# Column numbers of the count compares moved to PSUM, and layer 2's passes, row loads and way home paced anew, in a three-layer graph network kernel

## The chip, the cores and the metric

The kernel runs on one core of a Trainium2 chip. The metric is the device time of one execution in microseconds. The kernel before takes 2138.58 us (median of 3 runs, 2134.11 to 2144.74).

## The reference

A graph has 6250 nodes with 256 features and 100,000 edges, sorted by destination; every node also has an edge to itself. Three graph convolutions (256 to 512, 512 to 512, 512 to 256 features) each end in a relu. The input is added to the result, and each row is normalised.

```python
loops = jnp.arange(n)
src = jnp.concatenate([edge_index[0], loops]); dst = jnp.concatenate([edge_index[1], loops])
deg = segment_sum(ones_like(dst), dst, n)
dinv = where(deg > 0, rsqrt(deg), 0.0)
norm_edge = dinv[src] * dinv[dst]
for W, b in ((W1, b1), (W2, b2), (W3, b3)):
    h = relu(segment_sum((h @ W)[src] * norm_edge[:, None], dst, n) + b)
return layernorm(x + h)
```

## The kernel before, in words

The nodes are cut into 50 blocks (`NB`) of 125 (`Q`). A layer sums the rows of each block's sources in one of two ways.

**Gathered blocks.** GpSimd issues one indirect DMA per step (L1380, `room<-tab`): up to 128 rows of the layer's table in DRAM land in one buffer of a ring. A gathered block takes 14 "round" steps and 3 "beyond" steps, and some steps are shared by two or ten blocks. VectorE adds round rows to a running total (L1441). Beyond rows are split into a high and a low half by ScalarE (L1433) and VectorE (L1436), and TensorE multiplies them by a selection matrix (L1396).

**Dense blocks.** A 125 x 125 matrix of edge counts per pair of blocks is multiplied with the block rows that stay in SBUF (`parts`). In layers 1 and 3 the dense matmuls stand in L1464, behind a conversion of the counts from bytes (`converted`, L1348, on ScalarE and some on VectorE). In layer 2 the first 16 blocks are dense: four passes of four blocks each ("teams", L1193) run over all 50 block rows. Every unit of a pass needs the row halves (L1170 on ScalarE, L1172 on VectorE) and the counts, converted from bytes that SP reads back from DRAM (`room<-kept`, converted in L1160).

**The counts** are made in layer 1 (and for the last six blocks in layer 3) by `counts`. For four slots of 128 edges at a time VectorE compares slot values with column numbers: two instructions in L1041, one that writes 500 elements (125 node numbers, for two pairs of slots) and one that writes 1000 (250 keys). TensorE multiplies the two results (L1114), and ScalarE turns the sum into bytes (L1076). The column numbers (`runs`: each number twice, 16 bits each) lie in SBUF. Two steps go by per group of four slots.

**The finder** (`found_rounds`, `found_beyond`) works out, also during layer 1, which row each lane of a gather fetches. Its matmuls (L589, L598, L635, L647, L649) write columns 256 to 511 of the PSUM bank `near_cols`, and ScalarE reads them there (L593, L602, L637, L652). In layer 1 nothing uses columns 0 to 255 of that bank.

**Order.** All engines run in the order in which the program was written, without reordering. `layer` writes it step by step: the gather of this step, the work on rows gathered 3 to 6 steps earlier, the steps of finished blocks (`after1`, `after2`, `after3`), then a list of side jobs (`extras`), each a generator that says after how many steps it wants to go on, and then the dense matmuls that are due. Layer 1 has 423 steps, layer 2 599 and layer 3 317. The side jobs of layer 1 include the finder, then `counts`, then `caching`. `caching` brings layer 2's table rows into `parts`, two blocks per load (25 loads on SP); it begins when the dense blocks of layer 1 are finished, goes on while layer 1 drains, and then takes one load per step of layer 2.

**Layer 2's side jobs.** `teams` gives one yield per `PACE[1] / PACE[0]` parts of a unit: four parts (one per block, two matmuls each) per unit, 200 units. Twelve yields (`FRONT`) are taken ahead. A block that is finished goes through two matrix products (`after2`, L1594 and L1614) and is stored to `tab2`; as long as the teams run, it is not kept in SBUF, because `parts` still holds layer 2's rows. `home` brings these rows into `parts` when the teams have ended: runs of up to four blocks are loaded by SP (`parts<-tab`), and two turns later ScalarE and VectorE split them (L1220, L1222). When layer 2 drains, `ahead_of_time` puts 45 matmuls of layer 3's first dense block between (L1251).

```python
        for n in range(len(runs) + 2):
            if n < len(runs):
                b, e = runs[n][0], runs[n][-1] + 1
                by_rows(nc.sync, parts[:, b:e, C:].bitcast(F32), tables[2][b * Q:e * Q, :]...)
```

`by_rows` makes two DMAs of every load or store, one of 112 rows and one of 13.

Of the kernel before, what the change touches and what calls it, by code (L numbers as in the profile page):

```python
# [10 lines left out]
F32 = mybir.dt.float32  # L11
F32R = mybir.dt.float32r
BF16 = mybir.dt.bfloat16
# [10 lines left out]
P = 128  # L24
# [24 lines left out]
EXTRA = 0  # L49
TEAM = 4  # L50
TEAMS = 4
PACE = (2, 3)
FRONT = 12
MANY = 32
ALONE = 2
# [8 lines left out]
G = 5  # L64
# [3 lines left out]
RUN = 2  # L68
# [5 lines left out]
def by_rows(queue, tile_rows, dram_rows, store=False):  # L74

    for s in (slice(0, EVEN), slice(EVEN, Q)):
        if store:
            queue.dma_start(out=dram_rows[s], in_=tile_rows[s])
        else:
            queue.dma_start(out=tile_rows[s], in_=dram_rows[s])  # L80
# [320 lines left out]
def sorted_path(ctx: ExitStack, tc: tile.TileContext, x, edges, starts, found, wts, biases, room, late, out):  # L401
# [14 lines left out]
    nc = tc.nc  # L416
# [4 lines left out]
    N, C = x.shape  # L421
    HID = w1_sb.shape[2]
    EC = d.shape[1]
    NB = N // Q
# [328 lines left out]
    with tc.tile_pool(name="sdeg1", bufs=1) as dp1, tc.tile_pool(name="sdeg", bufs=2) as dp, \  # L753
# [26 lines left out]
        keys = const.tile([P, G * NB], BF16, name="keys")  # L780
# [183 lines left out]
    HW = -(-WIDE * (Q + G * NB) // 2 // 4) * 4  # L964
    hot_rooms = [room[:, 3 * MW + n * HW:][:, :HW].bitcast(BF16)[:, :WIDE * (Q + G * NB)] for n in range(HOMES)]
    first_rows = [room[:, at:at + C] for at in range(3 * MW + HOMES * HW, room.shape[1] - 4 * C - C + 1, C)]
    runs = room[:, room.shape[1] - 4 * C:][:, :G * NB * RUN // 2].bitcast(BF16).rearrange("p (v w) -> p v w", w=RUN)
    b1_rows = room[:3, room.shape[1] - 3 * C:][:, :C].bitcast(BF16)
    turned = [room[:, room.shape[1] - n * C:][:, :KC * Q].rearrange("p (k v) -> p k v", v=Q) for n in (2, 1)]
    pair = KH * 2 * Q  # L970
# [9 lines left out]
    def totals_of(stack, name, width, n_of):  # L980

        pool = stack.enter_context(tc.tile_pool(name=name, bufs=1))
        return [pool.tile([P, width], F32, name=f"total{n}") for n in range(n_of)]
# [11 lines left out]

    split = split_rows_of(one, "sfirst_split", 0, C)
    totals = totals_of(one, "sfirst_totals", C, 3)
    nc.vector.tensor_copy(runs, keys.unsqueeze(2).to_broadcast([P, G * NB, RUN]))
    bias_left = work.tile([Q, HID], F32, name="szs")[:3]
    nc.sync.dma_start(out=bias_left, in_=bass.AP(tensor=b1.tensor, offset=b1.offset, ap=[[0, 3], [1, HID]]))  # L1000

    ps_cols = ctx.enter_context(tc.tile_pool(name="sps_cols", bufs=1, space=bass.MemoryType.PSUM))
    near = ps_cols.tile([P, 512], F32, name="near_cols")
    ps_sum = ctx.enter_context(tc.tile_pool(name="sps_sum", bufs=1, space=bass.MemoryType.PSUM))
    accs = [ps_sum.tile([P, HID], F32, name=f"sacc{n}") for n in range(3)]
    mm_bank = ps_sum.tile([P, HID], F32, name="smm")
# [123 lines left out]
    stored, cached, at_home = set(), set(), set()  # L1130
# [3 lines left out]
    def caching():  # L1134

        while finished < FEW:
            yield 1
        for p in range(NB // 2):
            k = order[2 * p]
            while not {k, k + 1} <= rows_made:  # L1140
                yield 1
            by_rows(nc.sync, parts[:, k:k + 2].bitcast(F32), tables[1][k * Q:(k + 2) * Q, :].rearrange("(b p) c -> p b c", p=Q))
            cached.update((k, k + 1))
            yield 1

    def teams(groups):

# [34 lines left out]
        for u, (g, k) in enumerate(units):  # L1182
            for n, b in enumerate(groups[g]):
# [12 lines left out]
                if u % NB == NB - 1:  # L1196
                    team_ended[0](b, team_banks[n], f"team{n}")
                pace += PACE[0]
                while pace >= PACE[1]:
                    pace -= PACE[1]  # L1200
                    yield 1
        teams_done = True

    def home():

        while not teams_done:
            yield 1
        runs = []
        for b in sorted(waiting):
            if runs and runs[-1][-1] == b - 1 and len(runs[-1]) < 4:  # L1210
                runs[-1].append(b)
            else:
                runs.append([b])
        for n in range(len(runs) + 2):
            if n < len(runs):
                b, e = runs[n][0], runs[n][-1] + 1
                by_rows(nc.sync, parts[:, b:e, C:].bitcast(F32), tables[2][b * Q:e * Q, :].rearrange("(b p) c -> p b c", p=Q))
            if n >= 2:
                to = slice(runs[n - 2][0], runs[n - 2][-1] + 1)
                nc.scalar.copy(parts[:, to, :C], parts[:, to, C:].bitcast(F32))  # L1220
                yield 1
                nc.vector.tensor_sub(parts[:, to, C:], parts[:, to, C:].bitcast(F32), parts[:, to, :C].bitcast(F32))  # L1222
                at_home.update(runs[n - 2])
            yield 1

    rows_made = set()
# [451 lines left out]
    def other_parts():  # L1678
        for g, h in ((GRP, PIECE), (0, 0), (0, PIECE), (GRP, 0)):
# [5 lines left out]
            yield 1  # L1685

    loading = caching()
    team_work = teams([every[g * TEAM:(g + 1) * TEAM] for g in range(TEAMS)])
    def the_rest_found():
# [8 lines left out]
    def last_weights():  # L1698
# [11 lines left out]
    totals = totals_of(two, "swide_totals", HID, 2)  # L1710
    layer(1, HID, TEAM * TEAMS, [], after2, wide_rows,
          extras=[(5, last_weights()), (0, loading), (0, team_work), (20, home()), (steps(TEAM * TEAMS) - 2 * KF, fetch_first())],
          filler=ahead_of_time())
    assert begun % PIECE == 0
# [9 lines left out]
    runs = pairs.tile([P, G * NB, RUN], BF16, name="runs")  # L1724
# [6 lines left out]
def kernel(ctx: ExitStack, tc: tile.TileContext, x, edges, dst, w1, b1, w2, b2, w3, b3, out):  # L1731
# [133 lines left out]
    with tc.If(n_other == 0) as cmp:  # L1865
        sorted_path(tc, x, edges, starts, (d, nxt, ones, line, more, ends, other), (w1_sb, w2_sb, w3_sb), (b1, b2_sb, b3),
                    room, (load_x, late_w, load_w2, load_w3), out)
# [43 lines left out]
```

## Time and profile before

| | |
|---|---|
| profiled execution, its own time | 2139.47 us |
| its span, first to last instruction | 2137.7 us |
| median of 3 runs | 2138.58 us |
| layer 1: first gather to last gather issued | 105.6 to 771 us |
| layer 2 | 820.5 to 1671.3 us |
| layer 3 and the end | 1696.4 to 2137.7 us |
| busy: TensorE, VectorE, ScalarE, GpSimd | 86%, 73%, 54%, 70% of the span |

A profile's rows name source line, engine, operation, the tile written and those read. "POOL" is GpSimd, "DVE" VectorE, "ACT" ScalarE, "PE" TensorE (its weight loads "PEld"), "SP" the engine that issues most loads. In the table of stretches each engine's busy time is followed by its number of instructions, then come the granted TensorE clock (1.00 is full), the mean busy share of the DMA engines and GB/s. In rows of groups, the numbers behind the bar are the busy time, the mean duration of one in ns and the idle time of the engine before it. In rows of time, the first number is the start and the second the time taken, and brackets hold the idle time before.

### The profile page before, as it was taken

The numbers are of one execution on the slowest core, as the hardware profiler recorded it, in microseconds if no ns is written. First come the engines' busy times: TensorE is split into PE (matmuls) and PEld (weight loads), VectorE is DVE, ScalarE is ACT, GpSimd is POOL, SyncE is SP. The second block draws the span as 40 slices with busy tenths as digits, with TensorE's granted clock in tenths as the row PEclk, the third lists the DMA queues.
The fourth block names the chain that finished last, engine by engine and source line by source line (L and its number), as shares of the span: only waits on it lengthen the run. The fifth ranks groups of instructions, "written<-read, shape, count | busy, mean of one in ns | idle before, by whom it ended". The sixth has DMA issues, their size and how long they took to land. (4 is left out here: it accounts for less than half of the span.)

```text
span 2137.7 us, 29525 instructions
## 1 busy us (share of the span) xinstructions
PE 1840.7 (86%) x8487; PEld 1392.6 (65%) x8487; DVE 1565.7 (73%) x3299; ACT 1155.1 (54%) x2272; POOL 1503.1 (70%) x1382
## 2 busy tenths in 40 slices
PE   2548888989989995598999999999968799999996
PEld 1336655656656663476887787787756577777775
DVE  5699888878877733577668767767777378888877
ACT  0658767867867763344445444444443355555552
POOL 2088878877877734577777767777777477777775
PEclk6559999999999997799999999999988899999998
DMA  7434444444444549877767767777797467777884
GB/s 151 135 87 145 134 125 143 141 137 143 140 142 141 163 138 265 231 223 221 222 198 229 216 195 214 219 216 209 224 269 222 132 184 201 209 205 198 209 214 134
DMA packets 189676, 391.26 MB, mean 183 GB/s; under 512 B 43661, under 2 KB 105748, under 8 KB 189502
## 3 DMA queue, kind: packets, MB, share of 16 engines
q0 software_dynamic: 84816, 255.18, 42.3%
q1 hardware_dynamic: 88846, 122.24, 20.4%
q10 hardware_dynamic: 15840, 11.86, 2.3%
q8 instruction: 68, 1.11, 0.2%
q14 instruction: 106, 0.87, 0.1%
HBM read 332.12 MB, written 57.00 MB: 182 GB/s over the span
## 5 line engine op out<-in xcount | busy, mean ns | idle before, releaser
L1380 POOL DMA_INDIRECT room<-tab,round_src x1064 | 1166.0, 1096 | 439.3 <-issue 171.4
L1441 DVE TENSOR_TENSOR total<-total,room 125x256 f32<-125x256 f32 (+1 forms) x1030 | 551.7, 536 | 122.0 <-DMA room<-tab,round_src 107.1
L1348 ACT CAST piece<-room 125x625 fp32r<-125x625 uint8 x477 | 341.9, 725 | 110.6 <-PE win_ps L1464 28.8
L1380 POOL DMA_INDIRECT room<-tab,over_src x266 | 303.4, 1141 | 108.4 <-issue 43.3
L1172 DVE TENSOR_TENSOR both<-parts,both 125x512 fp32r<-125x512 f32 x200 | 137.9, 690 | 185.7 <-ACT both L1170 183.6
L1170 ACT CAST both<-parts 125x512 fp32r<-125x512 f32 x200 | 123.8, 619 | 269.8 <-PE smm L1193 269.2
L1464 PE MATMUL win_ps<-parts,piece 125*125 125x512 f32 x900 | 250.6, 417 | 0.5 <-ACT piece L1348 0.5
L1041 DVE TENSOR_TENSOR room<-room,slots 128x500 bf16<-128x500 bf16 (+1 forms) x326 | 247.9, 801 | 1.1 <-PE mat_ps L1114 1.1
L1433 ACT CAST halves<-room 128x256 fp32r<-128x256 f32 (+1 forms) x275 | 137.1, 504 | 177.6 <-DMA room<-tab,over_src 127.5
L1436 DVE TENSOR_TENSOR halves<-room,halves 128x256 fp32r<-128x256 f32 (+1 forms) x275 | 145.8, 541 | 94.4 <-ACT halves L1433 92.2
L1464 PE MATMUL smm<-parts,piece 125*125 125x512 f32 x705 | 193.4, 417 | 5.0 <-DVE piece L1348 5.0
L1193 PE MATMUL sacc<-both,team_piece 125*125 125x512 f32 x400 | 139.5, 425 | 64.2 <-ACT team_piece L1160 33.2
L1396 PE MATMUL sacc<-halves,shot 128*125 128x512 f32 x475 | 158.2, 430 | 39.1 <-ACT halves L1433 20.8
L1464 PE MATMUL mat_ps<-parts,piece 125*125 125x512 f32 x700 | 191.3, 413 | 0.0
L1464 PEld LDWEIGHTS win_ps<-parts,piece 125*125 125x125 f32 x900 | 160.7, 190 | 46.9 <-issue 12.1
L1114 PEld LDWEIGHTS <-room 128*125 128x125 bf16 x650 | 87.4, 144 | 107.4 <-issue 56.0
L1464 PEld LDWEIGHTS smm<-parts,piece 125*125 125x125 f32 x705 | 126.4, 191 | 36.5 <-DVE piece L1348 5.4
L1464 PE MATMUL sacc<-parts,piece 125*125 125x512 f32 x450 | 148.6, 444 | 0.0
L1464 PEld LDWEIGHTS mat_ps<-parts,piece 125*125 125x125 f32 x700 | 122.9, 187 | 35.5 <-issue 8.2
L1396 PEld LDWEIGHTS sacc<-halves,shot 128*125 128x125 f32 x475 | 93.4, 199 | 78.1 <-DVE halves L1436 31.0
L1160 ACT CAST team_piece<-room 125x500 fp32r<-125x500 uint8 x200 | 121.1, 605 | 38.2 <-DMA room<-kept 38.2
L1193 PE MATMUL mat_ps<-both,team_piece 125*125 125x512 f32 x400 | 134.9, 419 | 0.6 <-DVE room L1555 0.6
(416 smaller groups left out, 3306.3 us busy)
## 6 DMA issues: line engine op xcount, KB each, us to landing
kept<-room SPq DMA_DIRECT2D x32, 683.6 KB
room<-kept SPq DMA_DIRECT2D x32, 683.6 KB
room<-tab,round_src POOLq DMA_INDIRECT x1064
parts<-tab SPq DMA_DIRECT2D x34, 448.0 KB
tab<-st SPq DMA_DIRECT2D x58, 224.0 KB
room<-kept SPq DMA_DIRECT2D x160, 68.4 KB
room<-in_x SPq DMA_DIRECT2D x50, 112.0 KB
out<-st ACTq DMA_DIRECT2D x50, 112.0 KB
```

Of the source, the lines that this page charges most:

```text
L1041: nc.vector.tensor_tensor(out, runs[:, :shape[2], :shape[3]].unsqueeze(1).to_broadcast(shape), numbers.rearrange("p (s w) -> p s w", w=sha ...
L1160: nc.scalar.copy(team_pieces[u % 2], used_in[u // PIECE % 2][:, :, u % PIECE, :])
L1170: nc.scalar.copy(to[:, :HID], row)
L1172: nc.vector.tensor_sub(to[:, HID:], row, to[:, :HID].bitcast(F32))
L1193: nc.tensor.matmul(team_banks[n][:Q], lhsT=team_pieces[u % 2][:, n, :], rhs=both_parts[u % 2][:, h * HID:(h + 1) * HID], start=(u % NB == ...
L1348: convert(piece, made_or_read[:, c * PIECE:(c + 1) * PIECE, :])
L1380: nc.gpsimd.indirect_dma_start(out=row, out_offset=None, in_=tables[i], in_offset=bass.IndirectOffsetOnAxis(ap=at, axis=0))
L1396: nc.tensor.matmul(acc[:Q, :size], lhsT=hots[b][:, k], rhs=two[:, c0:c0 + size], start=(k == c0 == 0), stop=(k == BEYOND + 1 and c0 + size ...
L1433: nc.scalar.copy(two[:, :width], landed[chunk - hi_lag])
L1436: nc.vector.tensor_sub(two[:, width:], landed.pop(chunk - lo_lag), two[:, :width].bitcast(F32))
L1441: nc.vector.tensor_add(own, parts[:, b].bitcast(F32) if i == 1 and r == 0 else own, landed.pop(chunk - ADDED[i])[:Q])
L1464: nc.tensor.matmul(acc_d[:Q], lhsT=got[done // PIECE][:, k % PIECE, :], rhs=parts[:, k], start=(k == 0), stop=(k == NB - 1))
```

## The change

Three things are changed.

1. Before layer 1, the doubled column numbers are written to SBUF as before and then copied as 250 words of 32 bits to columns 0 to 249 of `near_cols`. Layer 1's compares (now L1043) take their first input from there. Their second input and their output stay in SBUF. Layer 3's compares are as before.
2. Layer 2's teams yield at 8/11 instead of 2/3 per part, and from the fifth load on `caching` waits four steps instead of one.
3. `home` goes through one run per step instead of two steps, and splits a run four turns after its load instead of two. A wait of one step between the split's two halves is gone.

```diff
-PACE = (2, 3)
+PACE = (8, 11)
...
-    runs = room[:, room.shape[1] - 4 * C:][:, :G * NB * RUN // 2].bitcast(BF16).rearrange("p (v w) -> p v w", w=RUN)
...
-    nc.vector.tensor_copy(runs, keys.unsqueeze(2).to_broadcast([P, G * NB, RUN]))
+    ps_cols = ctx.enter_context(tc.tile_pool(name="sps_cols", bufs=1, space=bass.MemoryType.PSUM))
+    near = ps_cols.tile([P, 512], F32, name="near_cols")
+    runs_room = room[:, room.shape[1] - 4 * C:][:, :G * NB]
+    nc.vector.tensor_copy(runs_room.bitcast(BF16).rearrange("p (v w) -> p v w", w=RUN), keys.unsqueeze(2).to_broadcast([P, G * NB, RUN]))
+    nc.vector.tensor_copy(near[:, :G * NB], runs_room)
+    runs = near[:, :G * NB].bitcast(BF16).rearrange("p (v w) -> p v w", w=RUN)
...
-    ps_cols = ctx.enter_context(tc.tile_pool(name="sps_cols", bufs=1, space=bass.MemoryType.PSUM))
-    near = ps_cols.tile([P, 512], F32, name="near_cols")
...
@@ caching
             cached.update((k, k + 1))
-            yield 1
+            yield 1 if p < 4 else 4
@@ home
-        for n in range(len(runs) + 2):
+        for n in range(len(runs) + 4):
             if n < len(runs):
...
-            if n >= 2:
-                to = slice(runs[n - 2][0], runs[n - 2][-1] + 1)
+            if n >= 4:
+                to = slice(runs[n - 4][0], runs[n - 4][-1] + 1)
                 nc.scalar.copy(parts[:, to, :C], parts[:, to, C:].bitcast(F32))
-                yield 1
                 nc.vector.tensor_sub(parts[:, to, C:], parts[:, to, C:].bitcast(F32), parts[:, to, :C].bitcast(F32))
-                at_home.update(runs[n - 2])
+                at_home.update(runs[n - 4])
             yield 1
```

## Prediction

> **What bounds the kernel now.** I read the table of stretches first, with one stretch per stage; the bounds differ between them. In order: layer 1 while the finder runs, the rest of layer 1, its drain, layer 2's start (two rows), its long middle, its steps after the teams, its drain, layer 3.
>
> ```profile
> 105.60:560.00 454.40, 385.66 (x2102) 263.88 (x2103) 390.46 (x938) 331.76 (x697) 365.18 (x284) 0.92 0.45 132
> 560.00:771.00 211.00, 193.53 (x822) 130.45 (x822) 154.75 (x315) 151.83 (x287) 166.80 (x146) 0.95 0.51 149
> 771.00:820.50 49.50, 31.25 (x119) 20.70 (x117) 3.40 (x8) 15.80 (x28) 0.67 (x1) 0.87 0.65 169
> 820.50:890.40 69.90, 38.49 (x139) 28.73 (x140) 30.23 (x47) 22.43 (x40) 36.05 (x35) 0.74 0.93 261
> 890.40:950.00 59.60, 55.38 (x234) 44.11 (x233) 46.13 (x72) 30.41 (x56) 45.79 (x45) 0.95 0.73 209
> 950.00:1563.60 613.60, 589.93 (x2628) 475.78 (x2628) 448.13 (x703) 297.89 (x562) 459.36 (x442) 0.99 0.75 216
> 1563.60:1671.30 107.70, 76.42 (x322) 61.76 (x320) 76.64 (x118) 34.36 (x65) 82.00 (x77) 0.84 0.85 241
> 1671.30:1696.40 25.10, 23.11 (x99) 17.45 (x99) 5.28 (x10) 10.70 (x20) 1.06 (x1) 0.81 0.39 108
> 1696.40:2137.70 441.30, 408.84 (x1796) 320.01 (x1795) 348.45 (x879) 224.92 (x410) 330.98 (x317) 0.97 0.72 191
> ```
>
> In layer 1 no engine looks full, so I asked for GpSimd's groups there (first three rows) and in layer 2's middle (last three).
>
> ```profile
> L1380 POOL DMA_INDIRECT room<-tab,round_src x336 | 406.0, 1208 | 125.3 <-issue 36.3 <-DVE parts L891 21.7 <-DVE room L1041 20.4
> L1380 POOL DMA_INDIRECT room<-tab,over_src x84 | 114.0, 1357 | 27.1 <-issue 8.2 <-DVE total L1441 6.1 <-DVE room L1041 5.2
> L1380 POOL DMA_INDIRECT room<-tab,rest x3 | 4.0, 1348 | 0.9 <-DVE room L1041 0.6 <-DVE ebegin L609 0.3
> ...
> L1380 POOL DMA_INDIRECT room<-tab,round_src x351 | 365.5, 1041 | 119.5 <-issue 84.2 <-DVE total L1441 15.9 <-DMA room<-tab,round_src 6.1
> L1380 POOL DMA_INDIRECT room<-tab,over_src x88 | 90.8, 1032 | 33.8 <-issue 21.0 <-DVE total L1441 9.1 <-DMA room<-tab,round_src 2.4
> L1380 POOL DMA_INDIRECT room<-tab,rest x3 | 3.0, 1002 | 0.9 <-issue 0.6 <-DMA room<-tab,round_src 0.3
> ```
>
> A gather takes 1239 ns on average in layer 1 (524.0 us over 423), 1039 in layer 2 (459.3 over 442). The rows in order of time show why. First VectorE and GpSimd around 641 us, then a pair from layer 2:
>
> ```profile
> 640.91 1.52 DVE L1041 TENSOR_TENSOR room<-room,slots 128x500 bf16<-128x500 bf16 x2
> 643.15 1.52 DVE L1041 TENSOR_TENSOR room<-room,slots 128x500 bf16<-128x500 bf16 x2
> 647.75 0.43 DVE L1436 TENSOR_TENSOR halves<-room,halves 128x256 fp32r<-128x256 f32 x1 [0.95 <-ACT halves L1433]
> 641.32 1.93 POOL L1380 DMA_INDIRECT room<-tab,over_src  x1 [0.30 <-DVE room L1041]
> 643.56 1.93 POOL L1380 DMA_INDIRECT room<-tab,over_src  x1 [0.30 <-DVE total L1441]
> 647.06 0.95 POOL L1380 DMA_INDIRECT room<-tab,over_src  x1 [0.31 <-DVE room L1067]
> ...
> 1095.65 0.74 DVE L1548 SCALAR_TENSOR_TENSOR szs<-sacc,sdinv,total 125x512 f32<-125x512 f32 x1
> 1096.13 0.95 POOL L1380 DMA_INDIRECT room<-tab,round_src  x1 [0.31 <-issue]
> ```
>
> A gather that begins while VectorE is idle takes 0.95 us and has 0.30 us before it. One that begins inside a compare (641.32, 643.56), which reads two inputs in SBUF, takes 1.93: it goes on when the compare ends. One that begins inside an instruction with one large input in PSUM and one in SBUF (1096.13, inside L1548) takes 0.95. So layer 1 is GpSimd's: 423 gathers at 0.95 + 0.30 are 529 us, the excess is 524 - 402 = 122, together 651 of the 666 us from 105.6 to 771. Layer 2's middle has GpSimd's chain (459.4 + 442 x 0.30 = 592 of 613.6 us) and TensorE (590) side by side at 96%.
>
> **Part 1, layer 1.** How much of the 122 us is the compares'? In layer 2's middle, with other two-input work and no compare, the excess is 459.3 - 442 x 0.95 = 39 us, 0.09 per gather; over 423 gathers 38. The compares have 122 - 38 = 84, at most 122. I take 85: 70 before 560 us (279 gathers), 15 after (144).
>
> How long the compares themselves take from PSUM no row shows. The nearest rows:
>
> ```profile
> L1041 DVE TENSOR_TENSOR room<-room,slots 128x1000 bf16<-128x1000 bf16 x162 | 193.5, 1194 | 0.0
> L1041 DVE TENSOR_TENSOR room<-room,slots 128x500 bf16<-128x500 bf16 x163 | 67.5, 414 | 1.1 <-PE mat_ps L1114 1.1
> L1441 DVE TENSOR_TENSOR total<-total,room 125x512 f32<-125x512 f32 x442 | 304.5, 689 | 46.3 <-DMA room<-tab,round_src 39.2
> L1441 DVE TENSOR_TENSOR total<-total,room 125x256 f32<-125x256 f32 x588 | 247.2, 420 | 75.6 <-DMA room<-tab,round_src 67.9 <-DMA total<-tab 1.8
> L1627 DVE TENSOR_TENSOR st<-str,sdinv 125x256 f32<-125x256 f32 x15 | 5.7, 417 | 0.0
> ```
>
> 256 elements from PSUM take what they take from SBUF (417, 420). From 256 to 512 elements the f32 rows grow by 269 ns, 1.05 ns each: 500 elements would take 676 at that rate, but the short compare takes 414, so it runs two elements at a time; the long one (1194 for 1000) runs one. Bounds from PSUM: 414 or 676 for the short, 676 or 1194 for the long. I take both unchanged, by the PSUM row that costs the same as SBUF's. At 676 the short ones add 163 x 0.26 = 43 us of VectorE work; at 676 the long ones remove 162 x 0.52 = 84. The Trainium skill, "VectorE: DVE Perf Modes", section "The perf-mode tier table (the rule you actually need)", gives tensor_tensor with any PSUM operand one element per cycle, while the section "Why PSUM operands drop a tier" below it still allows a packed rate of two. No 16-bit PSUM input is in this trace; the first sentence makes it a rival.
>
> What is late once the 85 us go? Before 560 us GpSimd's chain falls to 454 - 70 = 384, while VectorE has 390 us of work and TensorE 386. Layer 2's 96% on 390 gives 407. After 560, GpSimd falls to 196 and TensorE's 193.5 at 96% are 202, so -9.
>
> The change also adds waits. The columns share a bank with the finder's matmuls, and the built program guards by bank: counted in it, 75 compares wait for a ScalarE read of `near_cols`, 35 for a matmul into it, and 73 matmuls or weight loads of the finder wait for a compare. The compares are in VectorE's queue, with the adds (L1441) behind them that free gather buffers; the finder's matmuls hold the dense matmuls behind them. Where it is tightest, compare, matmul, ScalarE read and next compare form a ring per two steps:
>
> ```profile
> L635 PE MATMUL near_cols<-emarks,elow 128*128 128x256 bf16 x34 | 9.8, 289 | 16.9 <-DVE emarks L630 16.8
> L637 ACT ACTIVATE epast<-near_cols,eless 128x256 bf16<-128x256 f32 x34 | 16.4, 483 | 25.7 <-PE near_cols L635 25.6
> L1348 ACT CAST piece<-room 125x625 fp32r<-125x625 uint8 x477 | 341.9, 725 | 110.6 <-PE win_ps L1464 28.8
> ```
>
> 0.41 + 1.19 + 0.29 + 0.48 = 2.37 us, with half a cast (0.36) ahead of ScalarE's read 2.73. Two steps take 2 x 454.4 / 279 = 3.26 now and 2.92 at 407. The ring fits, barely; I charge 0.1 us for each of the 110 waits, some 12 us (bounds 0, and a whole cast each, 80). So 407 + 12 = 419, or -35. The one added copy to PSUM is under half a microsecond. Layer 1: -35 - 9 = **-44**. Its drain keeps its loads and stores: 0.
>
> **Part 2, layer 2.** At the start SP's loads of `parts` crowd out the teams' counts:
>
> ```profile
> 842.43 34.29 SPq L80 DMA_DIRECT2D parts<-tab  x16
> 881.01 56.35 SPq L80 DMA_DIRECT2D room<-kept  x40
> 888.38 1.22 PE L1193 MATMUL sacc<-both,team_piece 125*125 125x512 f32 x2 [22.42 <-ACT team_piece L1160]
> 890.45 1.28 POOL L1380 DMA_INDIRECT room<-tab,over_src  x1 [18.59 <-DVE total L1441]
> ```
>
> TensorE loses 22 us and GpSimd 19. Spread over 48 steps instead of 12, the 13 loads let the counts through. But up to 890 the DMA engines were 93% busy at 261 GB/s; the same bytes must pass, so only the idle time behind the loads' end (842.43 + 34.29 = 877) can come back. I take -8 (bounds -18 and 0).
>
> The middle: 800 parts at 8/11 instead of 2/3, less the 12 taken ahead, put the teams' last matmul into step 571, not 522. TensorE gets 2.75 instead of 3 of their matmuls per step, GpSimd's chain stays at 592 / 442 = 1.34 us per step. The step goes from 1.388 to about 1.36: 442 x 0.028 = -12 (bounds 0 and -21), and the 49 steps that had 107.7 / 77 = 1.40 give -2.
>
> The end: after the teams 28 steps are left instead of 77. `home` brings 42 blocks of 128 KB in 11 of them.
>
> ```profile
> parts<-tab SPq DMA_DIRECT2D x34, 448.0 KB
> ```
>
> With 0.45 MB per large load and 0.26 MB per gather (128 rows of 2 KB), the last 28 steps move 7.3 + 5.4 + 0.8 (first counts of layer 3) = 13.5 MB; at 241 to 261 GB/s (the stretch after the teams, and layer 2's start) that is 52 to 56 us, against 28 x 1.40 = 39 now: +14 (bounds 0, if the gathers wait less than the bytes say, and +17). Cover there is none: ScalarE and VectorE wait for these loads. The teams' last blocks now go through their matrix products while the layer drains; counted in the built program, 44 instead of 20 matmuls of L1594 and 16 instead of 8 of L1614.
>
> ```profile
> L1594 PE MATMUL win_ps<-room,w_sb 128*128 128x250 f32 x352 | 81.4, 373 | 0.0
> L1614 PE MATMUL str<-w,room 128*125 128x256 f32 x184 | 43.4, 379 | 0.5 <-ACT room L1605 0.5
> ```
>
> 24 x 0.23 + 8 x 0.24 = +7, as TensorE is 92% busy there; I take +6. Layer 2: -8 - 12 - 2 + 14 + 6 = **-2**.
>
> **The sum.** Against the profiled execution's own 2139.5 us: -44 - 2 = -46, 2093.5. The median is 0.9 lower: **2093 us**. About 0.5% (10.7 us) is what a measurement of this kernel can tell from no change.
>
> **Rivals.** (a) The short compares run one element at a time. VectorE's work before 560 us becomes 390 + 28 (two thirds of the 43, by its share of the time) = 418, at 96% and with the ring 447, -7; after it -9 stays: layer 1 -16, total 2121. Against it: L1627 reads PSUM at SBUF's pace. 17%.
>
> (b) The long compares run two at a time. Then GpSimd and TensorE bound: TensorE's 386 at 96% are 402 before 560 us, -52; with -9 and -2 that is 2076, and with layer 2 at its better bounds (-18 - 21 - 2 + 6) 2043. Nothing in the rows says why the long one is slow. 10%.
>
> (c) The compares are not what holds GpSimd. Layer 1 stays, the time is 2139 - 2 = 2137. The Trainium skill, "SBUF — State Buffer", section "Who interferes with whom", says that two SBUF inputs contend with GpSimd's reads, but reports a probe in which tensor_tensor did not stall DMAs issued by GpSimd. By the probe the sum would be -2, by the rows at 641 us it is -46. The trace decides against the probe: 9%.
>
> (d) Slower: the ring decides. It does from 3.26 us per two steps on, the present pace. If the gather's rows come late to ScalarE (L1433 stands in the same queue) or casts pile up, 3.6 us on 110 pairs are 110 x 0.34 = +37; with -9 and layer 2's -2 that is +26, 2165. For it: ScalarE already waits for the finder's matmuls (25.7 us before L637). Against it: each engine's other work per two steps (2.8 us) fits beside the ring. 14%.
>
> (e) Layer 2's burst costs more than the start and middle give: +30 there and -44 in layer 1, 2125. 5%.
>
> **How the numbers follow.** The forecast has 45%, at 2065 to 2125. Range: the lower end 2050 takes in most of (b); the upper end 2140 takes in (a), (c) and (e), and leaves out (d) and little else. Faster by over 0.5% (below 2128): the forecast but 1%, (b), most of (a), half of (e): 71%. Within: (c), the rest of (a) and (e), a little of (d): 13%. Slower: 16%.
>
> **What would show it.** Right: gathers in layer 1 near 1.04 us; L1043 at 414 and 1194 ns; last gather of layer 1 near 727 us; no 22 us hole before L1193; layer 2's drain some 30 us. Wrong: GpSimd's idle time in layer 1 put down to VectorE's adds, and waits of L1043 for L637 or of L635 for L1043 of over 40 us together (d); short compares near 676 ns (a); gathers still near 1.24 us (c).

## The result, and the profile after

The changed kernel takes 2143.66 us (median of 18 runs, 2135.91 to 2153.55), the kernel before 2135.43 us (18 runs, 2130.35 to 2144.74): ratio 1.0036, 95% interval 1.0021 to 1.0051. The forecast was 2093. The profiled execution of the changed kernel took 2138.86 us (span 2137.0), 4.8 below its median, so the two profiles, 0.6 us apart, show only where time moved.

In all experiments below but the last every kernel, the one before too, took 12 to 14% longer than in these runs (the last section shows what was seen of it), so ratios there are to runs of the kernel before that stood beside them on the same chip.

The table of stretches after the change, with the columns of the one before:

```profile
105.00:560.00 455.00, 370.55 (x1970) 256.05 (x1971) 374.77 (x892) 315.57 (x659) 277.75 (x273) 0.91 0.43 126
560.00:772.10 212.10, 203.41 (x940) 139.40 (x939) 168.25 (x356) 164.16 (x317) 154.78 (x157) 0.98 0.53 158
772.10:826.10 54.00, 35.14 (x136) 23.57 (x134) 5.90 (x14) 20.06 (x36) 0.93 (x2) 0.89 0.62 172
826.10:890.40 64.30, 49.63 (x164) 35.09 (x165) 39.58 (x61) 27.21 (x48) 46.36 (x46) 0.77 0.93 268
890.40:939.20 48.80, 45.12 (x197) 35.85 (x196) 37.24 (x58) 23.79 (x44) 37.21 (x36) 0.97 1.01 279
939.20:1615.00 675.80, 633.38 (x2791) 509.53 (x2790) 492.67 (x768) 312.16 (x587) 520.39 (x498) 0.98 0.75 218
1615.00:1660.30 45.30, 24.37 (x93) 19.33 (x92) 28.24 (x38) 17.94 (x28) 21.14 (x20) 0.74 0.90 243
1660.30:1694.30 34.00, 32.54 (x179) 27.86 (x177) 11.12 (x20) 14.92 (x33) 1.15 (x1) 1.00 0.33 97
1694.30:2137.00 442.70, 407.41 (x1795) 317.83 (x1795) 346.50 (x879) 222.62 (x410) 332.43 (x317) 0.97 0.72 190
```

Layer 1 lasts to 772 us (before: 771), though GpSimd is busy 433 us in it instead of 532. Layer 2 is 16.5 us shorter (834.3 for 850.8), its drain 8.9 longer, layer 1's drain 4.2 longer.

GpSimd's groups in layer 1, and after them VectorE's compares in the same stretch:

```profile
L1381 POOL DMA_INDIRECT room<-tab,round_src x336 | 339.4, 1010 | 199.0 <-issue 51.6 <-DVE total L1442 50.5 <-DVE parts L891 21.7
L1381 POOL DMA_INDIRECT room<-tab,over_src x84 | 83.3, 992 | 54.5 <-DVE total L1442 31.7 <-issue 8.5 <-DVE over_src L663 4.2
...
L1381 POOL DMA_INDIRECT room<-tab,rest x3 | 2.8, 943 | 0.9 <-DVE eplace L655 0.3 <-DVE total L1442 0.3 <-issue 0.3
```

```profile
L1043 DVE TENSOR_TENSOR room<-near_cols,slots 128x1000 bf16<-128x1000 bf16 x162 | 192.0, 1185 | 0.0
...
L1043 DVE TENSOR_TENSOR room<-near_cols,slots 128x500 bf16<-128x500 bf16 x163 | 67.7, 415 | 57.1 <-ACT epast L637 20.4 <-PE near_cols L635 11.4 <-ACT egot L602 7.7
```

The gathers went from 524.0 us to 425.5: of the excess of 122 us 98 are gone. The compares run at their old rate (1185 and 415 ns for 1194 and 414). But 57 us of idle time now stand ahead of them (1.1 before). The waits of layer 1 tell the rest (engine, line, who released it; us in total, times, longest):

```profile
POOL room L1381 <- DVE total L1442: 82.5, 105, 2.7
ACT epast L637 <- PE near_cols L635: 61.6, 35, 7.0
...
PE near_cols L635 <- DVE room L1043: 49.6, 23, 11.3
PEld L635 <- DVE room L1043: 46.6, 25, 11.4
...
DVE room L1043 <- ACT epast L637: 20.4, 25, 2.9
ACT epast L637 <- DVE room L1043: 19.5, 13, 2.5
...
PE near_cols L589 <- DVE room L1043: 13.7, 7, 3.6
DVE room L1043 <- PE near_cols L635: 11.4, 10, 2.2
```

All rows that join L1043 with L635, L637 or L589 are new: they are the shared bank. A part of them only takes the place of other waits. Before, TensorE waited for the compares at the matmuls that read their results (L1114):

```profile
PE sacc L1114 <- DVE room L1041: 23.8, 17, 10.3
...
PE mat_ps L1114 <- DVE room L1041: 5.6, 3, 3.5
...
PE smm L1114 <- DVE room L1041: 5.0, 3, 3.7
```

That is 34 us; after, these matmuls (L1116) wait 1 us for compares. With the finder's matmuls TensorE's waits for compares are 71 us in all, so 36 more than before. One turn of the shared bank, in order of time (start, duration, engine, in brackets the idle time before):

```profile
467.77 1.51 DVE L1043 TENSOR_TENSOR room<-near_cols,slots 128x500 bf16<-128x500 bf16 x2
469.20 0.87 DVE L1442 TENSOR_TENSOR total<-total,room 125x256 f32<-125x256 f32 x2
469.33 0.10 PEld L635 LDWEIGHTS <-elow 128*128 128x128 bf16 x1 [2.76 <-DVE room L1043]
469.34 0.28 PE L635 MATMUL near_cols<-emarks,elow 128*128 128x256 bf16 x1 [2.53 <-DVE room L1043]
...
469.66 0.47 ACT L637 ACTIVATE epast<-near_cols,eless 128x256 bf16<-128x256 f32 x1 [1.83 <-PE near_cols L635]
...
469.88 1.01 POOL L1381 DMA_INDIRECT room<-tab,round_src  x1 [1.87 <-DVE total L1442]
...
473.83 1.52 DVE L1043 TENSOR_TENSOR room<-near_cols,slots 128x500 bf16<-128x500 bf16 x2 [1.82 <-ACT epast L637]
```

The finder's matmul stands at the head of TensorE's queue for 2.53 us until both compares are through, and every dense matmul waits behind it. Two compares later VectorE waits 1.82 us for ScalarE's read. GpSimd, without a free buffer from 468.0 to 469.9, waits for an add that stood behind the compares.

The same kernel shows both cases. In the trace its first 280 gathers, with the finder running, take 476.0 us from first to last (before: 455.8, so +20.2); the other 143, mostly without the finder, 191.0 (before: 209.3, so -18.3). Between 600 and 700 us, when the finder is through, a step takes 1.32 us instead of 1.47.

### The profile page after: what moved, and what is told of

Its sections match the earlier page's. It is cut to its first block, busy times and chain, and to the rows that moved or that the text cites. A ratio compares the mean times of both kernels' runs of the same rounds, so it can differ in the third digit from the quotient of the medians.

```text
span 2137.0 us, 29508 instructions
## 1 busy us (share of the span) xinstructions
PE 1839.3 (86%) x8487; PEld 1394.2 (65%) x8487; DVE 1566.4 (73%) x3295; ACT 1153.4 (54%) x2269; POOL 1407.2 (66%) x1382
## 3 DMA queue, kind: packets, MB, share of 16 engines
q1 hardware_dynamic: 89317, 122.76, 20.4%
## 5 line engine op out<-in xcount | busy, mean ns | idle before, releaser
L1381 POOL DMA_INDIRECT room<-tab,round_src x1064 | 1099.2, 1033 | 529.1 <-issue 173.6
L1381 POOL DMA_INDIRECT room<-tab,over_src x266 | 275.9, 1037 | 113.9 <-issue 42.7
L1043 DVE TENSOR_TENSOR room<-near_cols,slots 128x500 bf16<-128x500 bf16 (+1 forms) x326 | 246.5, 797 | 57.1 <-ACT epast L637 20.4
L1195 PE MATMUL near_cols<-both,team_piece 125*125 125x512 f32 x400 | 135.1, 420 | 0.6 <-DVE room L1556 0.5
L1195 PE MATMUL smm<-both,team_piece 125*125 125x512 f32 x400 | 134.5, 418 | 1.1 <-DVE room L1556 1.1
```

Of the source, the lines that this page charges most:

```text
L1043: nc.vector.tensor_tensor(out, runs[:, :shape[2], :shape[3]].unsqueeze(1).to_broadcast(shape), numbers.rearrange("p (s w) -> p s w", w=sha ...
L1195: nc.tensor.matmul(team_banks[n][:Q], lhsT=team_pieces[u % 2][:, n, :], rhs=both_parts[u % 2][:, h * HID:(h + 1) * HID], start=(u % NB == ...
L1381: nc.gpsimd.indirect_dma_start(out=row, out_offset=None, in_=tables[i], in_offset=bass.IndirectOffsetOnAxis(ap=at, axis=0))
```

## The experiments

Four parts to take apart: columns in PSUM, the shared bank, layer 2's edits, and the long compares' slow rate.

**Each part alone, and a bank of its own.** The edits of part 1 alone and of parts 2 and 3 alone are the diff's. For a bank of their own the columns go to `tr_bank`, which the counts then lack; its control lacks the bank but keeps the columns in SBUF:

```diff
-SPARE = 1
+SPARE = 0
...
-    common += accs + [mm_bank, tr_bank, mat_bank]
+    common += accs + [mm_bank, mat_bank]
@@ own bank only
...
+    nc.vector.tensor_copy(tr_bank[:, :G * NB], runs_room)
+    runs = tr_bank[:, :G * NB].bitcast(BF16).rearrange("p (v w) -> p v w", w=RUN)
```

> Part 1 alone: column numbers in near_cols, layer 2 as before. Theory A (ring: the new waits between compare, finder matmul and ScalarE read in the shared bank set the step while the finder runs): gathers of layer 1 near 1.0 us on average, but the last gather of layer 1 again within 4 us of before's 771 us, since GpSimd waits for VectorE's adds instead; time 2135 to 2145, ratio 1.000 to 1.005. Theory B (layer 1 is neutral for another reason and the loss comes from layer 2's parts): ratio below 1.000. The forecast's step (layer 1 gains 44 us) would give 2090.

> Parts 2 and 3 alone: columns in SBUF as before, layer 2 paced as in the change. By the two profiles layer 2 goes from 850.8 to 834.2 us from first to last gather and its drain from 25.1 to 34.0, so -8 in all: 2124 to 2131, ratio 0.994 to 0.998, if the two parts simply add. If part 1's change of layer 1's end had brought the gain, or layer 2's parts are what costs: ratio 1.000 to 1.005.

> Before, with the column numbers in a PSUM bank of their own (tr_bank, which layer 1's other work then does without: six banks in turn instead of seven, and no bank held back). The finder's matmuls stay in near_cols, so compare and finder share no bank. Theory A (the shared bank's ring): neither gather nor ring holds the step, the finder's stretch falls from 1.63 to about 1.42 us per step and layer 1's last gather comes near 710 us; 2085 to 2100, if six banks cost little. Theory B (three engines with 390 us of work each cannot pack closer, bank or no bank): last gather again near 770. The kernel with six banks and columns in SBUF, run beside it, shows what the lost bank costs by itself.

> The control: before, with layer 1's other work in six banks as in the kernel with the columns' own bank, but the columns in SBUF. Both theories: gathers blocked by compares as before (about 1.24 us on average in layer 1), last gather near 771 us or some us later, 2135 to 2150. The difference between the two kernels is the columns' place alone.

Measured, as ratios to before: part 1 alone 1.0184 (1.0129 to 1.0239), parts 2 and 3 alone 0.9945 (0.9910 to 0.9980), own bank 1.0192 (1.0107 to 1.0278), its control 1.0064 (1.0022 to 1.0105). So in these runs part 1 costs, and more than either theory had said, and layer 2's edits gain. The own bank did not help, though its gathers took 1.01 us. Three of these were run again, with a fourth kernel for the long compares, whose second input begins on an odd 16-bit element; one more column in the tile moves it to a multiple of 4 bytes:

```diff
-    slots = const.tile([P, 2, NW * Q], BF16, name="slots")
+    slots = const.tile([P, 2, NW * Q + 1], BF16, name="slots")
```

> The kernel before, with layer 1's column numbers in PSUM as after, but in a bank of their own (the counts of layer 1 have six banks instead of seven, with the settings that suit six: none kept back, three at work). The gathers should take 1.00 us in layer 1, as in after. Theory R (what part 1 won went into the ring of compare, finder's matmul and ScalarE's read in one shared bank): the ring is gone, so VectorE no longer waits for ScalarE's read of near_cols ahead of a compare (after: 20.4 us), the stretch from 105 to 560 us holds over 295 gathers instead of 273, layer 1 ends some 40 us earlier than with six banks and the columns in SBUF, and the whole takes 2095 to 2115 us. Theory W (VectorE's and TensorE's own work sets the pace while the finder runs, with or without shared bank): gather 250 stays near 515 us and the whole near 2135.

> Control for the kernel with a bank of its own: the kernel before, columns in SBUF, with the same six banks and settings. Both theories: gathers at 1.24 us in layer 1, the whole within 0.7% of before (2121 to 2150 us).

> Part 1 alone: the columns in PSUM in the finder's bank, layer 2 as before. Theory R: gathers at 1.00 us, layer 1 and its drain as in after, 6 us longer than before (the waits of the shared bank cost as much as the contention did), layer 2 as before: 2140 to 2150 us. Rival (layer 2's part lost what part 1 won): layer 1 shorter than before, the whole near 2095.

> The kernel before with one column more in the tile slots, so that its second row, which the long compares read, begins on a multiple of 4 bytes instead of 2. Theory L (the long compares run one element at a time because one input begins off a 4-byte boundary): the long compare falls from 1194 to 680 ns or less, 84 us less of VectorE's work in layer 1, fewer gathers begin inside a compare, their mean in layer 1 falls to 1.15 us or less, and the whole to 2085 to 2115. Rival (the length or the pattern makes it slow): 1194 ns as before, 2135 us.

Own bank 1.0154 (1.0064 to 1.0244), control 1.0045 (1.0003 to 1.0087), part 1 1.0211 (1.0127 to 1.0296), aligned keys 1.0050 (1.0012 to 1.0088). The aligned long compare did fall, as its row shows, and with it the gathers to 1.08 us, but not the time:

```profile
L1041 DVE TENSOR_TENSOR room<-room,slots 128x1000 bf16<-128x1000 bf16 x162 | 109.2, 674 | 0.0
```

Then both whole kernels and two combinations of these edits:

> The kernel before itself, for a profile beside those of the same calls. Both theories: gathers at 1.24 us in layer 1, the time within 0.7% of the other runs of the kernel before in this call.

> The kernel after itself. Theory R (the waits of the shared bank cost what the contention did, layer 2 near nothing): 1.003 to 1.013 of before, as on record and as the product of parts 1 and 2 measured alone (1.0184 x 0.9945 = 1.013). Rival (the parts don't add up, one of them only costs beside the other): under 1.000.

> Before with the aligned keys and after's layer 2, columns in SBUF. If the long compares' faster rate is worth what VectorE saves before 560 us: 0.98 of before. If layer 1 doesn't go by VectorE or by GpSimd (as aligned keys alone at 1.005 speak for): layer 2's part alone, 0.994 to 1.000.

> Aligned keys, columns in PSUM in a bank of their own (six banks for the counts), and after's layer 2: no contention, no shared bank, 84 us less of VectorE work in layer 1. If layer 1 goes by GpSimd and VectorE: 0.96 to 0.98 of before, gather 250 below 490 us on an undisturbed chip. If it goes by the finder's chain (matmul, ScalarE, VectorE in turn) whatever the compares do: 1.00 to 1.01.

The kernel after 1.010 (1.003 to 1.0171), as the product of its parts (1.0184 x 0.9945 = 1.013): they add up. Aligned keys with layer 2's edits 1.002 (0.998 to 1.0061), with own bank too 1.009 (1.0053 to 1.0127). The profile of before from this set (2420.67 us) shows why none of these gained. Its layer 1, as one stretch, and its main gathers:

```profile
105.00:821.20 716.20, 586.37 (x2890) 399.17 (x2890) 545.05 (x1246) 475.75 (x967) 522.29 (x429) 0.93 0.43 126
```

```profile
L1380 POOL DMA_INDIRECT room<-tab,round_src x336 | 406.9, 1211 | 155.6 <-issue 63.5 <-DVE total L1441 24.6 <-DVE parts L891 21.7
```

GpSimd's chain is 522 + 423 x 0.30 = 649 of 716 us here, where by the same count it was 659 of 666. It was no longer the bound, so a shorter gather could become a longer wait. That is what the second pair of own bank and control shows: with six banks GpSimd's waits for the adds in layer 1 were

```profile
POOL room L1380 <- DVE total L1441: 54.8, 56, 7.0
```

and with the columns in a bank of their own

```profile
POOL room L1382 <- DVE total L1443: 147.3, 89, 7.3
```

92 us more, for the 96 that its busy time fell (528.7 to 433.1); and layer 1 took 752 us with the own bank, 736 with six banks.

**TensorE's load.** The next four kernels give TensorE less to do in layer 1:

```diff
-                    nc.tensor.matmul(acc_d[:Q], lhsT=got[done // PIECE][:, k % PIECE, :], rhs=parts[:, k],
+                    some = 256 if i == 0 and 0 < k < NB - 1 else 512
+                    nc.tensor.matmul(acc_d[:Q, :some], lhsT=got[done // PIECE][:, k % PIECE, :], rhs=parts[:, k, :some],
```

> The kernel before with TensorE relieved: in layer 1 the dense products (L1464) take only the first 256 of 512 columns, but for the first and the last block of a row. The control of the three others. TensorE falls well below the other engines in layer 1. Gathers at 1.2 us or over; GpSimd's chain (423 gathers at 0.95 + 0.30, and an excess of 100 to 120 us) sets layer 1: 635 to 660 us on every chip.

> The same relief with part 1 alone, columns in PSUM in the finder's bank. Theory R (the ring in the shared bank ate the gain): gathers at 1.00 us, but layer 1 at most 15 us shorter than with columns in SBUF, VectorE's waits for ScalarE's reads of near_cols and TensorE's for compares 60 us together or more. Rival Q (what ate the gain was TensorE's full queue behind the finder's matmuls; without it the ring fits): layer 1 down by 40 us or more, to about 600.

> The same relief with the columns in PSUM in a bank of their own, six banks for the counts. Theories R and Q: neither contention nor ring, GpSimd's chain is 423 x 1.25 + 20 = 550 and VectorE's work 545, so layer 1 takes 570 to 605 us, 45 us or more below the six-bank control. Rival C (the contention was not the bound, the finder's chain of matmul, ScalarE and VectorE is): as the control, 635 to 660.

> Control of the kernel with a bank of its own: the same relief, columns in SBUF, six banks for the counts. All theories: gathers at 1.2 us, layer 1 within 10 us of the relieved kernel with seven banks.

0.9981 (0.9946 to 1.0015), 1.0164 (1.0111 to 1.0216), 1.0183 (1.0130 to 1.0235), 0.9998 (0.9952 to 1.0043). Layer 1 took 706.5, 727.3, 733.1 and 715.7 us: every theory's number for the own bank was missed, and the kernel before, so relieved, took 706.5 where 635 to 660 had been expected. The relief was partial: TensorE's busy time in layer 1 was 514 us at a granted clock of 0.84, where the profile of before above has 586 us at 0.93. So it shows that less of it did not help, not that TensorE holds nothing there. A further run of the own bank gave the same again:

> The kernel before with the column numbers in PSUM in a bank of their own (six banks for the counts). On a chip where GpSimd's chain sets layer 1 (the kernel before near 2136 us): theory R, the ring, 2095 to 2115 us; theory W, VectorE's work and the finder's chain set the pace as soon as the gathers are quicker, 2130 to 2145. On a chip as in the calls before (the kernel before near 2400 us): 1.010 to 1.020 of before under both theories, gathers at 1.00 us, GpSimd's waits for VectorE's adds 100 us longer than with the columns in SBUF.

1.0151 (1.0076 to 1.0226).

**Everything removed at once.** The last run added to aligned keys, own bank and layer 2's edits one more step between ScalarE's copy of the finder's sums and VectorE's first use of it, in both functions:

```diff
         nc.scalar.copy(out_of, ways)
         yield
+        yield
```

> Aligned keys, columns in PSUM in a bank of their own and after's layer 2, as measured at 1.009 of before, and one step more between the finder's copies by ScalarE (L602, L652) and VectorE's first instruction on them (L605, L655). Theory V (VectorE's waits for these copies, with the adds behind them, set the pace): the waits before L655 and L605 fall from about 60 us to under 20, layer 1 by 30 us or more, the whole to 0.99 to 1.00 of before. Rival T (TensorE's late results hold everything behind them, whoever waits first): the waits move to other lines, layer 1 stays within 10 us, 1.005 to 1.015.

The longer finder also changes part of the computation: one pair of blocks now copies its sums (L602, at 105.4 us) only after other matmuls have been written over them in the same bank (L578 from 95.8 us on, L954 at 98.4), so its blocks can gather other rows. The count of gathers, bytes and instructions stays, so its time can be read, but it is no version to use. The kernel before took 2140.95 us beside it, as at the top, and this kernel 2072.35: 0.9698 (0.9659 to 0.9737), outside what both theories gave. It ran on the chip of the four kernels with less load, 80 minutes after them, and the delays that these theories are about were gone; so it does not tell theory V from T. It answers the older question. Its stretches of layer 1 and the drain, and the compares there:

```profile
105.00:560.00 455.00, 408.97 (x2211) 279.45 (x2211) 357.22 (x1004) 352.66 (x739) 313.03 (x311) 0.94 0.51 143
560.00:712.30 152.30, 150.26 (x695) 103.20 (x695) 103.83 (x253) 123.79 (x239) 114.81 (x118) 1.00 0.57 168
712.30:767.00 54.70, 35.81 (x139) 24.07 (x137) 5.90 (x14) 20.76 (x37) 0.94 (x1) 0.87 0.61 170
```

```profile
L1045 DVE TENSOR_TENSOR room<-str,slots 128x1000 bf16<-128x1000 bf16 x162 | 108.2, 668 | 0.0
L1045 DVE TENSOR_TENSOR room<-str,slots 128x500 bf16<-128x500 bf16 x163 | 66.9, 410 | 8.4 <-PE sacc L1118 4.6 <-PE win_ps L1118 2.0 <-PE smm L1118 1.4
```

Layer 1 takes 608.1 us, 59 less than after. The first 280 gathers take 418.1 us (after: 476.0), the others 190.0 (after: 191.0): all of the gain lies where the finder runs, and no compare waits for the finder any more. The gathers are as quick in both kernels (0.998 and 1.006 us). So where such delays are absent the time that the contention cost can be had, and after's 58 us more are not contention. Three edits differ there, however: own bank (with six banks for the counts), faster long compares (84 us of VectorE's work) and the later copies. How the 58 us divide among them no run shows.

## Why the prediction was wrong

**Contention: right.** The compares were said to cost the gathers 85 us of 122; with the columns in PSUM the gathers fell by 98. Rival (c) (9%), by which the compares are not what holds the gathers, is out. The Trainium skill, "SBUF — State Buffer", section "Who interferes with whom", says that two SBUF inputs contend with GpSimd's reads and one does not. These rows agree: 1239 ns a gather before, 1006 after.

**Rates: right.** 1185 and 415 ns, so rivals (a) and (b) are out, as such. That the long compare runs one element at a time I left unexplained; the runs give the reason, its input's address: 1194 ns, and 668 to 674 on a 4-byte boundary. The Trainium skill, "VectorE: DVE Perf Modes", section "Mode 2×_1P — pack two bf16 into one 32-bit read", asks for that alignment, and this measurement agrees. Another page of the Trainium skill, "Vector Engine (DVE) Microarchitecture Reference", section "5.1 Performance modes — why throughput varies by op and dtype", says that alignment makes no difference. In these compares, whose inputs are read as broadcasts, it does.

**What is late next: the step that failed.** The prediction gave the first 279 gathers 407 us and added 12 for the shared bank, 0.1 us for each of 110 waits. The stretch up to 560 us held 268 gathers in 455 us: 1.70 us a step instead of 1.50. Neither term of that sum held.

The 12 us: the ring was reckoned from its instructions' durations, 2.73 us against 2.92 for two steps, as if each engine were free when its turn came. None is: TensorE reaches the finder's matmul with two compares still queued on VectorE (2.53 us above), VectorE reaches the next compare before ScalarE has come to its read (1.82). In layer 1 TensorE waited 49.6 and 13.7 us for compares (L635, L589), and the compares 57.1 us for others, where the prediction had 12 in all. Even with the 34 us that TensorE used to wait for compares elsewhere taken off, that is far more than 12.

The 407 us: they rest on an engine that is busy 96% of the time, as in layer 2's middle. By the rows above, up to 560 us VectorE was busy 86% before (390 of 454 us) and 82% after (375 of 455). In the last run, without contention and shared bank and with 84 us less of compares, TensorE came to 90% (409 of 455), and the first 280 gathers still took 418 us. So no run shows 407. How the 57 us between 419 and 476 divide between the pace and the bank stays open, since the bank alone was taken away only where everything took longer, and there it gained nothing.

Its own mark for rival (d), waits of L1043 for L637 or of L635 for L1043 of over 40 us together, came true (20.4 and 49.6), and the 476 us lie inside its own bounds for the shared bank (407 to 487), far from the value taken. Rival (d) had the waits, at 14%. It let them begin with late reads by ScalarE, from 3.26 us per two steps on; in the turn above it is the finder's matmul that comes late, behind the compares. Its 2165 was too high by 21. The rival with the nearest time, (c) at 2137, had the wrong cause; its nearness is luck. With the finder through, the -9 became -18.

**Layer 1's drain** was put at 0 and took 4.2 us more. The difference stands ahead of the drain's first load of `parts`, which came 16.6 us behind the last gather instead of 11.8; what lagged there no run says.

**Layer 2: right in sign, small in size.** In the trace its first 50 steps take 71.0 us instead of 90.3 (-19; forecast -8, best bound -18), the next 520 take 707.8 instead of 722.3 (-14.5; forecast -14), the last 28 take 55.5 instead of 38.2 (+17; forecast +14) and the drain 34.0 instead of 25.1 (+9; forecast +6). Together -7.6 for -2. At the start the 22 us hole before the teams' matmuls is gone. The prediction held that the same bytes must pass before 890 us; they did not have to. By the tables, some 31 MB passed in 113 us (826 to 939), for 130 us before (820.5 to 950): the DMA engines moved 279 GB/s behind 890 us, where before they moved 209. Parts 2 and 3 alone, at 0.9945, are the only version here that was faster than before and can be used; alone they were measured only where everything took longer.

**The sum.** Forecast -46; the profiled pair shows +1.9 in layer 1, +4.2, -7.6 and +0.8 elsewhere, -0.7 us. The medians say +8.2; those further 9 us lie between executions, and this pair does not show in which stage.

## What to carry to other kernels

Before data moves into a memory bank that another chain uses, write down every pair of instructions that the bank now orders, and charge each pair with the wait of the engine that comes first in its own queue, with all that stands behind it, not with the ring's sum of durations. A share of busy time that engines reach in one stage is no forecast for another with other chains. A contention that is removed pays only while the engine that it delayed is the bound: add up that engine's chain first, and where it falls short of the stage, expect the gain to come back as a wait. And look at an input's address before its length: one more 16-bit column was worth 0.5 us in each long compare.

## What the runs showed of the hardware

Where everything took longer, engines began late on results of TensorE's. In that profile of before (2420.67 us), the finder's matmul and its reader:

```profile
412.76 0.27 PE L635 MATMUL near_cols<-emarks,elow 128*128 128x256 bf16 x1
...
418.90 0.47 ACT L637 ACTIVATE epast<-near_cols,eless 128x256 bf16<-128x256 f32 x1 [3.92 <-remote]
```

"remote" stands where no record in the trace explains the release. ScalarE's largest such group in that run, which the profiles of before, after and the last run do not have at all:

```profile
ACT both L1170 <- remote: 95.7, 20, 8.9
```

VectorE's and ScalarE's own instructions took what they took before, and giving TensorE's products half their columns changed little. But the traces differ in their records too: the profile of before at 2137.7 us holds 44,795 semaphore updates, this one 19,424, for the same 29,525 instructions, and all the longer runs hold less than half, in the same way. So a release without a known cause can also be one whose record is missing, and whether the results came late, their signals did, or the recording itself held engines up, no run shows. With these delays, kernels without the contention were not only no faster but 1 to 2% slower than their controls (own bank against six banks); why slower, and not equal, stays open too.
